# Middle weights of three outer products put by during attention, one piece per unit, instead of during the projections

## The chip, the cores and the metric

The kernel runs on one core of a Trainium2 chip. Its five engines each work through their own queue of instructions in order: TensorE (PE in the profile, PEld for its weight loads), VectorE (DVE), ScalarE (ACT), GpSimd (POOL) and SyncE (SP), which here only issues transfers. An instruction that has to wait holds up all that is queued behind it on its engine. The metric is device time in microseconds; three executions of the kernel before took 2657.4 to 2658.61 us, with a median of 2658.37 us.

## The reference

A transformer layer in float32 for 4 sequences of 512 tokens of width 1024: layer norm, then attention with 32 query heads in 8 groups (a bias by the square root of the distance, a causal mask) and, beside it, a linear layer with a routed low-rank part. Both are added to the input.

```python
x = hidden_states                                    # 4 x 512 x 1024
xn = _layernorm(x)
qkv = xn @ w_qkv                                     # 32 q heads, 8 k, 8 v, of 128
scores = einsum('bqhgd,bkhd->bhgqk', q, k) * scale + bias    # bias is -inf above the diagonal
attn = softmax(scores)
out = einsum('bhgqk,bkhd->bqhgd', attn, v).reshape(B, S, NH * D) @ w_o
lin = xn @ W.T + b
lora = the one of four low ranks (8, 16, 32, 64) that the gate picks for the token
return x + out + lin + lora
```

## The kernel before

The large products are not computed directly: each is cut into 2 x 2 blocks, and Winograd's form of Strassen's scheme makes 7 products of 8, at the price of sums of blocks before and after. In the projections this is done twice (7 outer products, each of 7 inner ones), in the last stage three times: outer, middle and inner. The work has three stages, one after another on TensorE:

- **projections** (to about 1121 us): for two pairs of sequences, 12 sets of columns each (`sets`: a k and v set, then two q sets), every set through its seven outer products. `item` is one outer product of one set; its seven inner products are the steps `m1` to `m7` of `Inner`, driven by `run`, which calls `beside` after each.
- **attention** (to about 1838 us): 32 units, one for a pair, a group of heads and a sequence. Tile rows `i` = 3, 2, 1, 0 of 128 queries have 512, 384, 256 and 128 keys to see. While unit n's probabilities are transposed and weighed with the values, the scores of unit n + 1 are made.
- **last stage**: `w_o` and the linear layer as one product, 7 outer times 7 middle products, `order` naming them as (outer, middle). Outer products are taken in the order 1, 2, 6, 5, 3, 7, 4.

The last stage needs sums of weight blocks. Those for the outer and middle level are made during the projections and put by in DRAM. One **piece** is a tile `wr` of four blocks of 128 x 256 (512 KB): it is loaded, four subtractions in a chain change it in place, and it is stored. There are 40 pieces of the outer level (keys `(kp, e, j)`, stored in `t_d`) and 70 of the middle level (keys `(kp, i)`, stored in `m_d[i]`, 10 for each outer product `i`). A middle piece of outer product 7, 4, 6 or 5 (`SUMMED`) is read from `t_d`, so it comes after the outer pieces; one of 1, 2 or 3 is read from the weights. The list `pieces` (L749 to L753) is shared by three generators `weights_put_by(turn)` (L756), each with a buffer `wr0`, `wr1`, `wr2`. The pieces alternate between GpSimd and VectorE. Loads are issued on ScalarE's queue, stores on SP's. Each `beside()` in the projections gives each of the three one step, in sets for which `pace[3]` is true. `pause(8)` therefore means eight steps between load and first subtraction, `pause(4)` four between last subtraction and store, and `pause(6)` six before the next load. GpSimd's own work there is the inner weights `ti` (L531), four subtractions before an inner product, and the sums over `r` (L582); VectorE's is reading the products out of PSUM (L130) and the sums of blocks.

In attention, `scores(u, i)` (L1004) does for each of four heads: a matmul into one of three banks of PSUM (`psc`, L1012), on VectorE a fused scale, bias and row minimum (`p`, `low`, L1017), on ScalarE the exponential (L1021). Then come the reciprocal (L1024) and, on GpSimd, the scaling of `p` (L1026). `transpose_probs` (L1032) transposes 128 x 128 blocks (`ptr`, L1037) and copies them out as `pt`, every other copy on VectorE (L1040). `weigh` (L1045) makes `po` (L1050). Unit n also loads `k`, `q` and `vT` of unit n + 2 (`load`, L965). Sums of the attention outputs for the last stage run beside: `outer_sums` (L1058) makes `os`, `middle_sums` (L1084) makes `ot`, and they are stored on SP's queue in `s_d` (L1103, L1104, L1114, L1116, L1117). `aside(steps, times)` (L1126) advances such a list by so many steps. In the unit loop (L1146) the calls stand at fixed places. `front[0]` (L1153), six units before the end, issues the first loads of the last stage (L1244, L1260, L1261).

In attention the order on TensorE and SP follows the program, as far as a transfer's buffer is free; that of the other engines is made by the scheduler, except that `pin` keeps what it is given in program order.

Of the kernel before, what the change touches and what calls it, by code (L numbers as in the profile page):

```python
# [23 lines left out]
G = NH // NKV  # L24
# [29 lines left out]
OUTER = (1, 2, 6, 5, 3, 7, 4)  # L54
# [5 lines left out]

SLOT = {1: 0, 7: 1, 2: 2, 4: 3, 5: 4, 6: 5, 3: 6}
SUMMED = {5: 0, 7: 1, 4: 2, 6: 3}


@with_exitstack
def kernel(
# [13 lines left out]
    nc = tc.nc  # L80
    B, S, H = x.shape
# [271 lines left out]
    def project(attention):  # L353
# [5 lines left out]
        with pool("a") as sb, tc.tile_pool(name="stats", bufs=2, reuse_waits="tile") as stats:  # L359
# [390 lines left out]
            for kp in range(2 * KB):  # L750
                if kp + 1 < 2 * KB:
                    pieces += [(kp + 1, e, j) for e in range(2) for j in range(2)]
                pieces += [(kp, i) for i in OUTER]  # L753
            put_by, taken = set(), {}

            def weights_put_by(turn):  # L756

                def load(key):  # L760
                    w = buf(f"wr{turn}", "wr_" + "_".join(str(k) for k in key))
                    if len(key) == 3:
                        kp, e, j = key
                        v = w.rearrange("p (k c) n -> p k c n", k=2)
                        for c in range(2):
                            pin(nc.scalar.dma_start(
                                out=v[:, :, c], in_=rows_of(kp, ds(c * S + j * HS, HS))[:, :, e]
                            ))
                    else:
                        kp, i = key  # L770
                        if i in SUMMED:
                            src = t_d[:, SUMMED[i], :, :, kp].rearrange("p e j n -> p (e j) n")
                            pin(nc.scalar.dma_start(out=w, in_=src))
                        else:
                            k, c = {1: (0, 0), 2: (1, 0), 3: (1, 1)}[i]
                            pin(nc.scalar.dma_start(
                                out=w.rearrange("p (e j) n -> p e (j n)", e=2),
                                in_=rows_of(kp, ts(c, S))[:, k],
                            ))
                    return w  # L780

                def busy(eng):

                    held = pace[2] > pace[4] if eng is GP else own_sums()
                    return held or taken.get(eng, -9) > pace[2] - 2

                yield from pause(9 * turn)
                for n in range(turn, len(pieces), 3):
                    key, eng = pieces[n], (GP, V)[n % 2]
                    if len(key) == 2 and key[1] in SUMMED:  # L790
                        while not put_by >= {(key[0], e, j) for e in range(2) for j in range(2)}:
                            yield
                    w = load(key)
                    yield from pause(8)
                    for k, u, v in ((0, 1, 0), (1, 3, 1), (3, 3, 0), (2, 2, 3)):
                        while busy(eng):
                            yield
                        taken[eng] = pace[2]
                        pin(sub(eng, w[:, k], w[:, u], w[:, v]))
                        yield  # L800
                    yield from pause(4)
                    if len(key) == 3:
                        kp, e, j = key
                        dst = t_d[:, :, e, j, kp]
                    else:
                        kp, i = key
                        dst = m_d[i][:, :, kp]
                    pin(nc.sync.dma_start(out=dst, in_=w))
                    put_by.add(key)
                    yield from pause(6)  # L810

            def once(f, *args):
                f(*args)
# [2 lines left out]
            def pause(n):  # L816
                for _ in range(n):
                    yield
# [122 lines left out]
    def attend(front, begin):  # L941
# [3 lines left out]
        with ExitStack() as stack:  # L945
            sb, sq = None, early.__enter__()
            units = [(p, h, bi) for p in range(NP) for h in range(NKV) for bi in range(2)]
            sizes = {"dist": (S,), "q": (G, S), "k": (S,), "vT": (S,), "bias": (G, S)}
            counts = {"q": 2, "k": 2, "vT": 2, "v": 2, "pt": 10, "o": 4, "ot": 2}
            for i in (3, 2, 1, 0):  # L950
                sizes[f"p{i}"] = (G, (i + 1) * P)
                counts[f"p{i}"] = 2
            sizes.update(v=(NT, D), pt=(S,), os=(3, 2, S), o=(G, S), ot=(9, HS))
            queries = ("dist", "q", "k", "vT", "bias")

            def buf(tag, name):
                where = sq if tag in queries else sb
                return where.tile([P, *sizes[tag]], F32, tag=tag, name=name, bufs=counts.get(tag, 1))
# [6 lines left out]
            def load(u, queue=nc.sync):  # L965
                p, h, bi = u
                n = label(u)
                K[u] = buf("k", f"k_{n}")
                Q[u] = buf("q", f"q_{n}")
                VT[u] = buf("vT", f"vT_{n}")  # L970
                queue.dma_start(out=K[u], in_=k_d[2 * p + bi, h - h % 2][:, h % 2])
                queue.dma_start(out=Q[u], in_=q_d[2 * p + bi, h])
                queue.dma_start(out=VT[u], in_=v_d[2 * p + bi, h - h % 2][:, h % 2])
# [145 lines left out]
            def pause(n):  # L1119
                for _ in range(n):  # L1120
                    yield
# [4 lines left out]
            def aside(steps, times):  # L1126
                while steps and times:
                    times -= 1
                    if next(steps[0], True):
                        steps.popleft()  # L1130

            fill = iter(())
            for u in units[:2]:
                load(u)
# [11 lines left out]
            for n, u in enumerate(units):  # L1146
                p, h, bi = u
                nxt = units[n + 1] if n + 1 < len(units) else None
                after = units[n + 2] if n + 2 < len(units) else None
                if after:  # L1150
                    load(after)
                if n == len(units) - 6:
                    front[0]()  # L1153
                if not nxt:
                    early.__exit__(None, None, None)
                    front[1](O[p, h, 0])
                    fill = begin()
                if bi == 1:
                    beside.append(middle_sums(p, h, (1, 2), "o", O[p, h, 0], True))
                for i in (3, 2, 1, 0):  # L1160
                    if nxt:
                        scores(nxt, i)
                    if i > 1:
                        aside(outer, 1)
                    aside(below, 2)
                    if i < 2 or not nxt and i < 3 or n == close - 2 and i == 2:
                        aside(beside, 2)
                    if i < 2:
                        weigh(u, i + 2)
                        if i == 0 and not nxt:  # L1170
                            outer_sums(p, h, slice(HS, S))
                        next(fill, None)
                    transpose_probs(u, i)
                    next(fill, None)
                    if i == 2 and nxt:
                        values(nxt)
                    if i == 3:
                        aside(outer, 1)
                    if not nxt:
                        if i == 3:  # L1180
                            aside(beside, 2)
                        if i == 2:
                            while beside:
                                aside(beside, 1)
                        if i < 2:
                            front[3 - i]()
                if after and after[2] == 0:
                    distances(after)
                aside(beside, 2)
                weigh(u, 1)  # L1190
                next(fill, None)
                weigh(u, 0)
                if n == close:

                    while beside:
                        aside(beside, 1)
                for _ in fill:
                    pass
                if bi == 1:
                    if n + 1 == close:  # L1200
                        o = O[p, h, 1]
                        outer.append(outer_steps(p, h))
                        aside(outer, 1)
                        t = OS[p, h]
                    else:
                        o, t = outer_sums(p, h, slice(0, HS if (p, h) == last else S))
                        beside.append(pause(3))
                        for k in range(2):
                            O.pop((p, h, k))
                        OS.pop((p, h))  # L1210
                    below.append(middle_sums(p, h, (7, 4), "o", o, False))
                    beside.append(middle_sums(p, h, (5, 6, 3), "os", t, False))
            aside(beside, 9)
            aside(below, 9)
            assert not (beside or below)

    def rows_of(kp, col):

# [506 lines left out]
```

## Time and profile before

| | us |
|---|---|
| median of three executions | 2658.37 |
| the profiled execution | 2657.69 |
| its span, from first to last instruction | 2655.9 |
| DVE `wr<-wr` in the projections | 110 + 110 rows at 128x256, mean 0.645 |
| POOL `wr<-wr` in the projections | 110 + 110 rows at 128x256, mean 0.786 |
| POOL `ti_q<-w_q` at 128x256 | 0.827 mean |
| TensorE, all instructions | busy 2600.1 |

The 220 rows of each engine are two groups of 110 that the page adds up. The first subtraction of a piece starts at 118.2 us and the last at 1088.0 us. The granted TensorE clock is 0.996 over the span. Bytes over the span: 392.72 MB read and 261.10 MB written, 246 GB/s. The issue table of the page gives the median time from issue to landing: 4.6 us for `m<-wr`, 3.7 for `t<-wr`, 6.7 for `wr<-t` and 5.7 for the 512 KB `wr<-in_w_o_dram`.

A row of a timeline is: start us, us, engine, line, operation, tiles written `<-` read, shape, count, and in brackets the idle time of the engine before it and what ended it. A row of stages is: from:to us, its length, then for PE, PEld, DVE, ACT and POOL the busy time and number of instructions, the granted clock, the share of the DMA engines and GB/s. A row of waits is: who waited for whom, us in total, times, longest. Lines are those of the kernel before.

### The profile page before, as it was taken

The numbers are of one execution on the slowest core, as the hardware profiler recorded it, in microseconds if no ns is written. First come the engines' busy times: TensorE is split into PE (matmuls) and PEld (weight loads), VectorE is DVE, ScalarE is ACT, GpSimd is POOL, SyncE is SP. The second block draws the span as 40 slices with busy tenths as digits, with TensorE's granted clock in tenths as the row PEclk, the third lists the DMA queues.
The fourth block names the chain that finished last, engine by engine and source line by source line (L and its number), as shares of the span: only waits on it lengthen the run. The fifth ranks groups of instructions, "written<-read, shape, count | busy, mean of one in ns | idle before, by whom it ended". The sixth has DMA issues, their size and how long they took to land.

```text
span 2655.9 us, 35975 instructions
## 1 busy us (share of the span) xinstructions
PE 2600.1 (98%) x11872; PEld 2074.8 (78%) x11872; DVE 1797.7 (68%) x3654; ACT 652.1 (25%) x1730; POOL 1921.4 (72%) x1976
## 2 busy tenths in 40 slices
PE   7899999999999999999999999999999999999999
PEld 7788888888888888866666666665788888888887
DVE  6876776778676767566666666666766666666574
ACT  3011111100000000276666666675000000000000
POOL 2588787877798989667777778675765567755593
PEclk9999999999999999999999999999999999999999
DMA  4379897858876767336666575766987888878884
GB/s 139 104 264 310 281 349 230 295 193 315 286 256 205 264 223 254 129 102 208 226 205 226 186 229 188 226 238 223 363 287 285 301 293 327 283 277 311 308 319 175
DMA packets 386570, 656.19 MB, mean 247 GB/s; under 512 B 22441, under 2 KB 291113, under 8 KB 376274
## 3 DMA queue, kind: packets, MB, share of 16 engines
q1 hardware_dynamic: 314322, 566.47, 61.5%
q10 hardware_dynamic: 70752, 82.85, 9.6%
q0 software_dynamic: 1312, 4.59, 0.5%
q8 instruction: 95, 1.56, 0.2%
q14 instruction: 89, 0.73, 0.1%
HBM read 392.72 MB, written 261.10 MB: 246 GB/s over the span
## 4 chain that ended last, share of the span: by engine, by line
PE 65%; POOL 4%; DVE 3%; DMA 3%; issue 1%; SPq 1%; ACT 0%; POOLq 0%; ACTq 0%; DVEq 0%
PE pc L1308 15%; PE psc L1012 9%; PE po L1050 8%; PE pd L1308 8%; PE pc_q L553 6%; PE pa L1308 4%; PE pc_kv L553 3%; PE ptr L1037 3%; PE pd_q L553 3%; PE pd_kv L553 2%; PE pa_q L553 1%; DMA s<-os 1%; DVE p L1017 1%; DVE pt L1040 1%; PE pa_kv L553 1%
## 5 line engine op out<-in xcount | busy, mean ns | idle before, releaser
L1026 POOL TENSOR_SCALAR p<-p,tot 128x256 f32<-128x256 f32 (+3 forms) x512 | 319.8, 643 | 139.4 <-DVE tot L1024 89.0
L1012 PE MATMUL psc<-k,q 128*128 128x512 f32 (+3 forms) x1024 | 306.3, 437 | 3.0 <-DVE low L1017 1.7
L1017 DVE CUSTOM_DVE_ANT_0 p<-psc,bias 128x256 f32<-128x256 f32 (+3 forms) x512 | 244.7, 491 | 93.3 <-PE psc L1012 70.4
L1021 ACT ACTIVATE p<-p,low 128x256 f32<-128x256 f32 (+3 forms) x512 | 284.4, 557 | 74.7 <-DVE low L1017 63.0
L1050 PE MATMUL po<-pt,v 128*128 128x512 f32 x640 | 290.9, 593 | 0.7 <-DVE pt L1040 0.7
L133 POOL TENSOR_TENSOR t<-w 128x640 f32<-128x640 f32 x95 | 183.1, 1927 | 134.4 <-DMA w<-m 60.6
L1012 PEld LDWEIGHTS psc<-k,q 128*128 128x128 f32 x1024 | 172.5, 190 | 102.5 <-issue 54.5
L133 POOL TENSOR_TENSOR t<-w,t 128x640 f32<-128x640 f32 x95 | 196.0, 2063 | 35.2 <-PE pc L1308 31.4
L1037 PEld LDWEIGHTS ptr<-ident,p 128*128 128x128 f32 x1280 | 147.5, 141 | 71.4 <-issue 39.0
L1050 PEld LDWEIGHTS po<-pt,v 128*128 128x128 f32 x640 | 116.7, 190 | 109.7 <-issue 99.5
L133 POOL TENSOR_TENSOR wr<-wr 128x256 f32<-128x256 f32 x220 | 172.5, 786 | 32.8 <-DMA wr<-in_w_o_dram 10.4
L1040 DVE COPY pt<-ptr 128x512 f32<-128x512 f32 x192 | 130.0, 684 | 76.0 <-PE ptr L1037 74.1
L1037 PE MATMUL ptr<-ident,p 128*128 128x128 f32 x1280 | 167.6, 274 | 4.4 <-DVE pt L1040 3.0
L553 PE MATMUL pc_q<-xi,ti_q 128*128 128x256 f32 x640 | 166.6, 383 | 3.1 <-DVE q L130 2.0
L168 ACT COPY m<-pc 128x256 f32<-128x256 f32 x30 | 11.2, 373 | 564.3 <-PE pc L1308 560.0
L133 POOL TENSOR_TENSOR ti_q<-w_q 128x256 f32<-128x256 f32 x128 | 105.9, 827 | 58.7 <-PE pc_kv L553 35.4
L133 DVE TENSOR_TENSOR wr<-wr 128x256 f32<-128x256 f32 x220 | 141.9, 645 | 6.1 <-DMA s<-xo 3.1
L553 PEld LDWEIGHTS pc_q<-xi,ti_q 128*128 128x128 f32 x640 | 120.2, 191 | 24.4 <-issue 7.5
L553 PE MATMUL pd_q<-xi,ti_q 128*128 128x256 f32 x448 | 116.1, 381 | 7.1 <-POOL ti_q L133 7.1
L168 ACT COPY q<-pc_q 128x256 f32<-128x256 f32 x64 | 23.8, 373 | 359.6 <-PE pc_q L553 311.2
L1308 PE MATMUL pc<-sa,w 128*128 128x256 f32 x480 | 112.1, 381 | 0.0
L1308 PE MATMUL pd<-s,w 128*128 128x256 f32 x480 | 111.5, 379 | 0.0
(343 smaller groups left out, 6016.8 us busy)
## 6 DMA issues: line engine op xcount, KB each, us to landing
sa<-s SPq DMA_DIRECT2D x98, 640.0 KB, 7.9
s<-ot SPq DMA_DIRECT2D x107, 384.0 KB, 4.8
m<-wr SPq DMA_DIRECT2D x70, 512.0 KB, 4.6
w<-m SPq DMA_DIRECT2D x28, 1280.0 KB, 7.1
w_q<-in_w_qkv_dram SPq DMA_DIRECT2D x16, 2048.0 KB, 12.4
q<-q SPq DMA_DIRECT2D x32, 1024.0 KB, 7.2
s<-os SPq DMA_DIRECT2D x45, 512.0 KB, 4.7
t<-wr SPq DMA_DIRECT2D x40, 512.0 KB, 3.7
```

The source lines that it names most:

```text
L133: return eng.tensor_tensor(dst, u, v, ALU.subtract)
L168: nc.scalar.copy(dst, src)
L553: nc.tensor.matmul(dst, ops_w[m][:, c, :], XI[i][m][:, c, :], start=start and c == 0, stop=c == 1, skip_group_check=True,)
L1012: nc.tensor.matmul(sc[:, :n], Q[u][:, g, ts(i, P)], K[u][:, :n], start=True, stop=True)
L1017: nc.vector.tensor_tensor_reduce(pr[:, g], sc[:, :n], bias[p, h][:, g, S - n :], -SCALE, BIG, ALU.add, ALU.min, low,)
L1021: nc.scalar.activation(pr[:, g], pr[:, g], AF.Exp, bias=low, scale=-1.0, accum_out=tot[:, g : g + 1])
L1026: nc.gpsimd.tensor_scalar(pr[:, g], pr[:, g], tot[:, g : g + 1], 1.0, ALU.mult, ALU.mult)
L1037: nc.tensor.transpose(tr[:, ts(g, P)], PR[u, i][:, g, ts(j, P)], ident)
L1040: nc.vector.tensor_copy(pt, tr)
L1050: nc.tensor.matmul(po, V[u][:, j, :], PT[i, j], start=(j == 0), stop=(j == i))
L1308: nc.tensor.matmul(bk, w[:, k], x[:, k], start=start and k == 0, stop=stop and k == KB - 1, skip_group_check=True,)
```

## The change

The thirty middle pieces of outer products 3, 7 and 4 leave the list of the projections. A new generator makes them in attention, all on VectorE, with one buffer `wr` of its own, its loads and stores both on SP's queue. It is stepped six times in each of the first 31 units: once after `load` (the load), twice after the transposes of tile row 1 and twice after those of tile row 0 (the four subtractions), and once at the end of the unit (the store). The 80 pieces that stay in the projections still go by turns to three generators, with pauses of 14, 5 and 10 steps in place of 8, 4 and 6.

```diff
+LATE = (3, 7, 4)
...
-                pieces += [(kp, i) for i in OUTER]
+                pieces += [(kp, i) for i in OUTER if i not in LATE]
...
                     w = load(key)
-                    yield from pause(8)
+                    yield from pause(14)
...
-                    yield from pause(4)
+                    yield from pause(5)
...
-                    yield from pause(6)
+                    yield from pause(10)
...
-            sizes = {"dist": (S,), "q": (G, S), "k": (S,), "vT": (S,), "bias": (G, S)}
+            sizes = {"dist": (S,), "q": (G, S), "k": (S,), "vT": (S,), "bias": (G, S), "wr": (4, HS)}
...
-            queries = ("dist", "q", "k", "vT", "bias")
+            queries = ("dist", "q", "k", "vT", "bias", "wr")
...
+            def late_weights():
+
+                for kp, i in [(kp, i) for i in LATE for kp in range(2 * KB)]:
+                    w = buf("wr", f"wr_{kp}_{i}")
+                    if i in SUMMED:
+                        src = t_d[:, SUMMED[i], :, :, kp].rearrange("p e j n -> p (e j) n")
+                        nc.sync.dma_start(out=w, in_=src)
+                    else:
+                        nc.sync.dma_start(
+                            out=w.rearrange("p (e j) n -> p e (j n)", e=2), in_=rows_of(kp, ts(1, S))[:, 1]
+                        )
+                    yield
+                    for k, s, t in ((0, 1, 0), (1, 3, 1), (3, 3, 0), (2, 2, 3)):
+                        pin(sub(nc.vector, w[:, k], w[:, s], w[:, t]))
+                        yield
+                    nc.sync.dma_start(out=m_d[i][:, :, kp], in_=w)
+                    yield
+
+            pieces = deque([late_weights()])
...
                     load(after)
+                if nxt:
+                    aside(pieces, 1)
...
                     transpose_probs(u, i)
+                    if nxt and i < 2:
+                        aside(pieces, 2)
...
                 for _ in fill:
                     pass
+                if nxt:
+                    aside(pieces, 1)
```

More of the change, by code (lines that the diff above doesn't have):

```diff
@@ L1214, in attend @@
             aside(below, 9)
-            assert not (beside or below)
+            assert not (beside or below or pieces)
     def rows_of(kp, col):
```

## The prediction

> **What bounds the kernel now.** I read the shares of busy time first, then the busy time by stage, then who waited for whom in each stage, and last the timeline of single units.
>
> ```profile
> span 2655.9 us, 35975 instructions
> PE 2600.1 (98%) x11872; PEld 2074.8 (78%) x11872; DVE 1797.7 (68%) x3654; ACT 652.1 (25%) x1730; POOL 1921.4 (72%) x1976
> 133.00:598.00 465.00, 455.74 (x2187) 395.17 (x2185) 341.92 (x729) 61.63 (x133) 382.76 (x473) 1.00 0.81 274
> 598.00:1121.00 523.00, 515.41 (x2365) 447.06 (x2364) 359.79 (x722) 40.28 (x103) 437.77 (x544) 1.00 0.71 243
> 1121.00:1838.00 717.00, 709.63 (x3002) 433.59 (x3001) 487.10 (x1459) 490.11 (x1361) 528.03 (x628) 1.00 0.62 201
> ```
>
> TensorE is the bound everywhere: it idles 9.3 + 7.6 = 16.9 us in the projections from 133 us on, and 7.4 us in attention. So the change can win at most some 17 us, plus matmuls that are stretched without showing as idle; whatever it puts before a matmul in attention is lost in full. VectorE is busy 68% of attention, with gaps of about 7 us in a unit of 22.8 us. Who holds TensorE up in the projections:
>
> ```profile
> PE pd_q L553 <- POOL ti_q L133: 7.1, 9, 1.3
> PE pd_q L553 <- DVE q L130: 2.1, 4, 0.7
> PE pc_q L553 <- DVE q L130: 2.0, 4, 0.7
> ```
>
> [...]Half is GpSimd making the inner weights late, half VectorE reading PSUM late.
>
> **Gain in the projections.** In the changed program's own order a set of projections holds 8 piece subtractions on GpSimd where there were 11 or 12, and 8 on VectorE where there were 11 or 12: 160 each instead of 220. I walked the timeline back from each of the 31 idle stretches of TensorE over 0.06 us between 133 and 1121 us (16.7 us in sum). About 10 us have a piece's subtraction among the last instructions ahead of the one waited for; about 6 us are led by the sums over `r` or the outer sums, which stay. Of the 10 us, three stretches (0.86, 0.97, 0.64 us at 672, 674 and 686) follow a subtraction that itself stood waiting for a transfer:
>
> ```profile
> 668.96 2.33 POOL L133 TENSOR_TENSOR wr<-wr 128x256 f32<-128x256 f32 x3 [4.80 <-DMA wr<-t]
> 672.02 1.13 PE L553 MATMUL pd_q<-xi,ti_q 128*128 128x256 f32 x4 [0.86 <-POOL ti_q L133]
> ```
>
> A pause of 14 steps instead of 8 between load and first subtraction takes these away: 2.5 us. The other 7.5 us shrink with the count, by 60/220: 2.0 us. Each such stall also stretches its matmuls by 0.1 to 0.3 us (1.13 against 1.03 for four), about 1.5 us in all. Gain **6 us**; from 2 (waits only move) to 12 (most go). The 30 loads that ACT no longer issues free 30 x 0.37 us of an engine busy 25%: nothing. The weights concerned are first read at the 29th of 49 last-stage items, some 450 us after attention: being stored later costs nothing.
>
> **Cost in attention: the order on VectorE.** Thirty pieces of four subtractions are 120 x 0.41 to 0.67 us = 50 to 80 us. That VectorE has room for it (230 us idle) says little, since it works in order. The changed order puts the first subtraction right after the copy `pt` of tile row 1 and before the first minimum of the four `i = 0` score heads, the second after that minimum, the last two after the unit's last `pt`. At the first place:
>
> ```profile
> 1444.60 0.69 DVE L1040 COPY pt<-ptr 128x512 f32<-128x512 f32 x1 [0.63 <-PE ptr L1037]
> 1444.83 1.27 PE L1012 MATMUL psc<-k,q 128*128 128x128 f32 x8
> 1445.26 0.29 DVE L1017 CUSTOM_DVE_ANT_0 p<-psc,bias 128x128 f32<-128x128 f32 x1
> 1448.52 0.60 PE L1037 MATMUL ptr<-ident,p 128*128 128x128 f32 x4
> ```
>
> Scores have three banks, so the fourth head needs the first head's minimum done. Eight matmuls that flow take 0.28 + 7 x 0.107 = 1.03 us (four transposes of the same width: 0.60 = 0.28 + 3 x 0.107); these take 1.27, in the units between 1.38. The fourth head is thus **already waiting** for VectorE, with no slack, in every unit: what stands before that minimum moves TensorE one for one. Engines overlap successive instructions by some 0.08 us, and in every second unit VectorE has 0.08 us to spare, so a subtraction of 0.41 us delays by 0.2 to 0.35 us.
>
> Here a rule speaks against the change. The Trainium skill, "SBUF — State Buffer", section "Who interferes with whom": a VectorE instruction with two SBUF inputs contends with a GpSimd instruction that reads SBUF, and the later one blocks for the whole of the other. GpSimd is scaling `p` (128x384 or 128x256) at this point in 26 of 32 units. The trace agrees in the projections: pieces on VectorE average 0.417 us with GpSimd idle (23) and 0.67 us beside its two-input work (196). Beside scaling by 128x128 a 128x512 sum of attention takes 0.727 us against 0.679 alone. By that row the delay stays near 0.3 us, 9 us in all; by the rule half of a 0.6 us scaling comes on top, 0.55 us, 16 us. I take 0.4 us: 30 x 0.4 = **12 us**, kept between 6 and 17.
>
> The second subtraction is covered: ScalarE paces what follows (four exponentials, 0.39 us apart, against 0.22 us of minima). The last two have 1.49 or 0.84 us of VectorE idle before the next unit's first minimum, and its fourth head another 0.8 us: nothing, at worst 0.2 us in half the units.
>
> **The new wait: landing.** That first subtraction also waits for the piece's load, and everything in VectorE's queue, hence the fourth head, waits behind it. The load waits for the previous piece's store to land (one buffer). In SP's new order the store of one unit kind stands behind four stores and before `k` and `q`: it is issued at about 1455, lands at 1460, the load lands by 1466, the subtraction stands at 1468: in time. In the other kind it stands late:
>
> ```profile
> 1477.20 1.19 SPq L972 DMA_DIRECT2D q<-q  x1
> 1478.49 0.93 SPq L1104 DMA_DIRECT2D s<-o  x2
> 1479.51 1.26 SPq L1103 DMA_DIRECT2D s<-o  x2
> 1484.67 0.33 SPq L973 DMA_DIRECT2D vT<-v  x1
> 1488.00:1490.00 2.00, 2.00 (x9) 0.99 (x8) 1.65 (x2) 0.16 (x1) 1.90 (x2) 1.00 0.00 0
> ```
>
> The store goes between L1104 and L1103, at 1479.5, into queues that are full at 333 to 344 GB/s until 1486; half a megabyte adds 1.5 us. It lands at about 1486.5, the load is issued then, and the subtraction is due at 1490.9. The page's issue table gives 4.6 us for `m<-wr` and 6.7 for `wr<-t` under load; the shortest here is 3.2. "DMA: Bandwidth & Descriptors", section "Anatomy of one DMA", fits 2.0 us + bytes / 436 kB per us (for GpSimd's path): 3.2 us, lands at 1489.7, no wait; by 4.6 us it lands at 1491.1, 0.2 us late; by 6.7, 2.3 us late. As the queues have just run dry I stay near the first two: 14 units x 0.15 = **2 us**; ends 0 and 14 x 2 = 28. `vT`, queued behind this load, is due a unit later: free.
>
> Near the end of attention SP runs late and last-stage loads fill the queues. At 1757 store, `k`, `q` and `vT` precede the load, which then lands near 1767.5, due at 1765.3: 2 us. Two units on, SP's new order puts the load behind six stores of `os` and `ot` that before are issued from 1805 to 1811.7:
>
> ```profile
> 1808.66 1.39 SPq L1116 DMA_DIRECT2D s<-os  x1
> 1810.09 1.56 SPq L1117 DMA_DIRECT2D s<-ot  x1
> ```
>
> It is issued at about 1812.5 and, behind a backlog (the last store took 7.9 us), lands near 1819; the subtraction is due at 1811.4. That is 7 to 8 us, of which 2 us fall on a wait that VectorE has there anyway. Together **8 us**, from 0 to 12. The last-stage loads, moved behind a piece's load from 1714 to about 1739, are needed after 1838: nothing.
>
> **Sum.** -6 + 12 + 2 + 8 = +16 us. The profiled execution took 2657.7 us (span 2655.9), 0.7 below the median of 2658.4; so about **2674 us**, its own range 2664 to 2684.
>
> **Rivals.** (1) *The pieces fit VectorE's gaps and the projections run free*: for it, 230 us idle in attention; then gains of 6 to 12 us stand alone against at most 4: 2650. Against it, the 1.27 us row. Chance 0.10. (2) *Draw*: the subtraction delays 0.25 us (7 us), all loads land, the projections give 8: 2658. Chance 0.15. (3) *Landing decides*: in every second unit the load comes 1.5 us late, so 12 + 21 + 10 - 6 = +37: 2695. It decides from a load time above 4.4 us on, and `wr<-t` has 6.7. Chance 0.20. Or the freed slots give nothing in the projections, since waits move to the sums over `r`: 2680, inside the forecast's range. Forecast 0.55.
>
> Measurement tells about 0.2% (5.3 us) from no change. Faster 0.10, same 0.15, slower 0.75. The range runs from the draw to rival 3, 2655 to 2695.
>
> **What would show it.** TensorE idle in the projections falls from 16.9 to 11 to 13 us. In attention the eight 128x128 score matmuls take about 1.7 us, and VectorE's `wr` rows wait for `DMA wr` little except in the last four units. Attention lengthens by some 20 us. If the score row stays near 1.3 us, my main step is wrong; if `wr` waits for DMA in every second unit, rival 3 is right.

## The result, and the profile after

The changed kernel takes 2667.87 us (median of six executions, 2665.2 to 2670.49), the kernel before, run beside it, 2657.89 us (2654.64 to 2662.27). The ratio is 1.0036, with a 95% interval of 1.0023 to 1.0049: **slower**, by less than half a per cent but clear of 1, and by 10 us where 16 were forecast. The profiled execution's span is 2666.6 us, 10.7 us above that of before.

The head of the page, then the rows by stage in the windows used for before:

```profile
span 2666.6 us, 35927 instructions
PE 2601.0 (98%) x11872; PEld 2078.4 (78%) x11872; DVE 1813.8 (68%) x3714; ACT 654.9 (25%) x1730; POOL 1874.1 (70%) x1916
133.00:598.00 465.00, 457.57 (x2200) 397.60 (x2199) 325.36 (x705) 61.84 (x133) 354.67 (x441) 1.00 0.72 240
598.00:1121.00 523.00, 520.03 (x2393) 452.35 (x2392) 353.41 (x710) 46.81 (x119) 418.46 (x529) 1.00 0.64 218
1121.00:1838.00 717.00, 694.24 (x2930) 423.21 (x2929) 517.10 (x1538) 479.43 (x1323) 518.92 (x609) 1.00 0.73 242
```

TensorE's busy total is the same within 1 us, so the shares tell nothing; the rows by stage do. In the two rows up to 1121 us it idles 7.4 + 3.0 = 10.4 us where it idled 16.9; in attention it idles 22.8 us where it idled 7.4. Who it waits for, first in the projections, then in attention (1121 to 1850 us), and last the row of the kernel before for the same wait in attention:

```profile
PE pd_q L555 <- POOL ti_q L135: 3.3, 5, 1.2
PE pc_q L555 <- DVE q L132: 2.0, 3, 0.9
```

```profile
PE psc L1014 <- DVE low L1019: 18.2, 32, 3.7
PE ptr L1039 <- DVE pt L1042: 2.9, 15, 0.2
```

```profile
PE psc L1012 <- DVE low L1017: 1.7, 3, 0.9
```

The wait for GpSimd's `ti_q` has halved from 7.1. The new wait is that of a score matmul for VectorE's row minimum: once for each of the thirty pieces, one of these as long as 3.7 us, and two at the end that the kernel before has as well. One unit of the middle, all engines but with most lines left out, shows the place:

```profile
1371.82 2.61 POOL L1028 TENSOR_SCALAR p<-p,tot 128x384 f32<-128x384 f32 x4
1371.92 0.69 DVE L1042 COPY pt<-ptr 128x512 f32<-128x512 f32 x1 [2.34 <-PE ptr L1039]
1372.16 0.83 PE L1014 MATMUL psc<-k,q 128*128 128x128 f32 x6
...
1372.53 0.70 DVE L135 TENSOR_TENSOR wr<-wr 128x256 f32<-128x256 f32 x1
1373.16 0.28 DVE L1019 CUSTOM_DVE_ANT_0 p<-psc,bias 128x128 f32<-128x128 f32 x1
...
1373.50 0.49 PE L1014 MATMUL psc<-k,q 128*128 128x128 f32 x2 [0.51 <-DVE low L1019]
```

Three heads' matmuls (six) flow; those of the fourth (two) stand 0.51 us until the first head's minimum is done, and that stood behind the piece's subtraction. The eight matmuls that took 1.27 us in the prediction's unit now take 1373.99 - 1372.16 = 1.83 us. The subtraction takes 0.70 us, not the 0.41 of one that is alone, and GpSimd is scaling `p` all the while.

Where the 10.7 us come from, read at fixed matmuls of the two traces:

| stretch on TensorE | before, us | after, us | change |
|---|---|---|---|
| start to the set of projections that begins near 112 us | 111.52 | 114.51 | +3.0 |
| from there to the last matmul of the projections | 1011.08 | 999.81 | -11.3 |
| first to last score matmul | 716.63 | 735.40 | +18.8 |
| last score matmul to the end | 818.57 | 818.76 | +0.2 |

The third stretch begins 1.9 us before the second ends, in both kernels. The first row has nothing to do with the change: it is the clock, and is told under the hardware below.

### The profile page after: what moved, and what is told of

It reads as the page before. It is cut to its first block, busy times and chain, and to the rows that moved or that the text cites. A ratio compares the mean times of both kernels' runs of the same rounds, so it can differ in the third digit from the quotient of the medians.

```text
span 2666.6 us, 35927 instructions
## 1 busy us (share of the span) xinstructions
PE 2601.0 (98%) x11872; PEld 2078.4 (78%) x11872; DVE 1813.8 (68%) x3714; ACT 654.9 (25%) x1730; POOL 1874.1 (70%) x1916
## 4 chain that ended last, share of the span: by engine, by line
PE 69%; DVE 3%; DMA 2%; issue 1%; POOL 0%; SPq 0%; ACT 0%; DVEq 0%; ACTq 0%; POOLq 0%
PE pc L1336 15%; PE po L1052 10%; PE psc L1014 9%; PE pd L1336 8%; PE pc_q L555 7%; PE pa L1336 4%; PE pd_q L555 3%; PE pc_kv L555 3%; PE ptr L1039 3%; PE pa_q L555 2%; PE pd_kv L555 2%; DVE p L1019 1%; DVE pt L1042 1%; PE pa_kv L555 1%; PE ptr_v L1003 1%
## 5 line engine op out<-in xcount | busy, mean ns | idle before, releaser
L1028 POOL TENSOR_SCALAR p<-p,tot 128x256 f32<-128x256 f32 (+3 forms) x512 | 328.4, 662 | 162.8 <-DVE tot L1026 107.6
L1014 PE MATMUL psc<-k,q 128*128 128x512 f32 (+3 forms) x1024 | 306.9, 437 | 18.7 <-DVE low L1019 18.2
L135 DVE TENSOR_TENSOR wr<-wr 128x256 f32<-128x256 f32 x280 | 164.3, 587 | 4.6 <-DMA wr<-t 3.6
L135 POOL TENSOR_TENSOR wr<-wr 128x256 f32<-128x256 f32 x160 | 124.8, 780 | 6.4
L135 POOL TENSOR_TENSOR ti_q<-to_q 128x256 f32<-128x256 f32 x96 | 72.0, 750 | 63.8 <-PE pc_q L555 61.5
L135 POOL TENSOR_TENSOR ti_q<-w_q,ti_q 128x256 f32<-128x256 f32 x128 | 113.1, 883 | 5.0
```

The lines of the kernel that those rows point to most:

```text
L135: return eng.tensor_tensor(dst, u, v, ALU.subtract)
L1014: nc.tensor.matmul(sc[:, :n], Q[u][:, g, ts(i, P)], K[u][:, :n], start=True, stop=True)
L1028: nc.gpsimd.tensor_scalar(pr[:, g], pr[:, g], tot[:, g : g + 1], 1.0, ALU.mult, ALU.mult)
```

## The experiments

All runs were timed beside the kernel before. It took 2659.9 us (2652.95 to 2664.31) beside the two other places, the run without subtractions and the one with the old pauses; 2659.64 (2654.55 to 2662.38) beside the two doses and the run without late pieces; and 2659.51 (2652.02 to 2664.98) beside the other three. Each was profiled once. "Attention" is the time from the first to the last score matmul; "pitch" is the mean distance of the units 3 to 28, measured from one unit's first score matmul to the next one's: 22.85 us in the kernel before, 23.30 in the changed one.

**Is it the order? Two other places for the first two subtractions.** In the first run they are made after the first head's minimum:

```diff
-            def scores(u, i):
+            def scores(u, i, between=lambda: None):
...
+                    if g == 0:
+                        between()
...
-                        scores(nxt, i)
+                        scores(nxt, i, (lambda: aside(pieces, 2)) if i == 0 else lambda: None)
...
-                    if nxt and i < 2:
+                    if nxt and i < 1:
                         aside(pieces, 2)
```

> The same 120 subtractions, loads and stores; only the first pair of each unit stands one place later on VectorE: behind the first head's minimum instead of ahead of it. Theory A (order: what stands ahead of the first minimum of the 128-key scores holds up the fourth head's matmul): the eight 128x128 score matmuls go back from 1.7 us with a stall to about 1.3 us, a unit gets 0.4 us shorter, 28 units give 12 us: attention about 723 us instead of 735, the kernel about 2655 to 2657 us. Theory B (amount: VectorE and GpSimd block each other, wherever the subtractions stand): nothing changes, 2667. Theory C (the added megabyte of transfers per unit): nothing changes, 2667.

In the second they come once all of the 128-key row's minima and its reciprocal are done:

```diff
                         scores(nxt, i)
+                        if i == 0:
+                            aside(pieces, 2)
...
-                    if nxt and i < 2:
+                    if nxt and i < 1:
                         aside(pieces, 2)
```

> The first pair stands behind all four minima of the 128-key scores and the reciprocal, ahead of the last pt copy of the unit. Theory A: as in the run before for the score matmuls, and the load has 2 us more to land, so that the one late unit near the end costs 1 to 2 us instead of 4; but in every second unit the pt copy now stands behind two sums and two subtractions and may come late for the last weighing, 0 to 0.5 us in 15 units. 2652 to 2662 us. Theories B and C: 2667.

The first took 2655.88 us, ratio 0.9989 (0.9978 to 1.0000), hardly told from the kernel before; attention 722.4 us, pitch 22.84. The second took 2655.10 us, ratio 0.9975 (0.9966 to 0.9985), **faster than both kernels**; attention 719.3, pitch 22.86. TensorE's waits in attention in the second:

```profile
PE ptr L1039 <- DVE pt L1042: 2.9, 15, 0.2
PE psc L1014 <- DVE low L1019: 2.0, 3, 0.9
PE po L1052 <- DVE pt L1042: 1.7, 2, 1.1
```

The 18.2 us are gone, with as many subtractions and transfers as in the changed kernel. Here is how little their own duration matters at a good place:

```profile
1370.66 0.18 DVE L1026 RECIPROCAL tot<-tot 128x4 f32<-128x4 f32 x1 [0.84 <-ACT p L1023]
1370.75 1.91 DVE L135 TENSOR_TENSOR wr<-wr 128x256 f32<-128x256 f32 x2
```

The two take 1.91 us here, beside two-input sums on GpSimd, against 0.8 alone, and the pitch does not show it: nothing that TensorE needs soon is queued behind them. So the place is the cause of the regular delay, and the amount and the transfers are not. What the first variant still loses is the last piece, whose load is late by 4.47 us:

```profile
1808.99 0.43 DVE L135 TENSOR_TENSOR wr<-wr 128x256 f32<-128x256 f32 x1 [4.47 <-DMA wr<-t]
1813.22 1.10 PE L1054 MATMUL po<-pt,v 128*128 128x512 f32 x2 [3.43 <-DVE pt L1044]
```

**A miss: no subtractions at all.** This was meant to have only the transfers in attention:

```diff
-                        pin(sub(nc.vector, w[:, k], w[:, s], w[:, t]))
```

> Leaves out the 120 subtractions in attention; the pieces are still loaded and stored at the same places of SP's queue (what is stored is the raw blocks). Theory A: attention goes back to about 717 us, the kernel to about 2649 us. Theory B: the same, 2649. Theory C: attention stays near 735 us, the kernel near 2667.

It took 2709.26 us, ratio 1.0185 (1.0171 to 1.0199). The waits of SyncE's queue and of TensorE in attention say why:

```profile
SPq L1148 <- DMA wr<-t: 60.1, 14, 6.8
SPq L1140 <- DMA m<-wr: 42.5, 13, 5.6
...
PE psc L1014 <- DMA q<-q: 23.9, 5, 8.5
PE psc L1014 <- DVE low L1019: 16.3, 9, 4.2
```

With no arithmetic between load and store, the planned order of SyncE's queue put load, store and load of pieces next to each other. SyncE then stood for each landing, `q` queued behind it came late, and TensorE waited 8.5 us at worst. How the other 16.3 us, behind VectorE's minima, come about was not followed. The run tests nothing of what it was made for; it shows what a transfer that waits costs when it stands ahead of one that is needed.

**The dose.** So the subtractions were kept, with their waits and places, and only shortened: to one column, and to half of the columns.

```diff
-                        pin(sub(nc.vector, w[:, k], w[:, s], w[:, t]))
+                        pin(sub(nc.vector, w[:, k, :1], w[:, s, :1], w[:, t, :1]))
```

```diff
-                        pin(sub(nc.vector, w[:, k], w[:, s], w[:, t]))
+                        pin(sub(nc.vector, w[:, k, :HS // 2], w[:, s, :HS // 2], w[:, t, :HS // 2]))
```

> The changed kernel with each of the 120 late subtractions cut to one column (128x1 in place of 128x256): this leaves out nearly all of their arithmetic, and keeps every load, store, wait and the order of all queues. Theory A (the time of the first subtraction ahead of the first 128-key minimum is what attention pays): the fourth score head flows again but for a fixed cost of an instruction of some 0.06 us; unit pitch about 22.9 us, attention 718 to 723 us, of which 3 to 6 are the last piece's late landing; total about 2652. Theory C (the 30 MB of loads and stores in attention is what it pays): attention stays at 735, total 2668. A mixture would lie between.

> As the run with one column, but each late subtraction works on 128 of the 256 columns: half of the arithmetic left out, all queues and waits as in the changed kernel. A dose test. Theory A: a subtraction of 128x128 takes about 0.2 us, so the fourth score head waits about half as long, 0.2 to 0.25 us a unit: attention 724 to 729 us, total about 2659 to 2662, midway between the run with one column and the changed kernel. If the cost were a step that does not depend on the length (a switch or block of VectorE by GpSimd), attention would stay at 733 to 736; if it were the transfers, likewise.

One column: 2659.25 us, ratio 0.9999 (0.9990 to 1.0008), attention 727.9. Half: 2661.98 us, ratio 1.0013 (1.0004 to 1.0022), attention 728.8. Theory C, attention at 735 us whatever the length, falls: the transfers cost TensorE time only where a load is late (0.85 us in one unit of the middle and some 4.4 us in the last two of the run with one column). Theory A holds in direction, and in the second run in size, but one column was to cost next to nothing and costs over two fifths of the full subtraction. The first subtraction of a unit, from the three timelines, in the units where GpSimd is scaling beside it and in those few where it is not:

| columns | alone, us | beside scaling (median), us | pitch over before, us |
|---|---|---|---|
| 1 | 0.155 | 0.402 | 0.20 |
| 128 | 0.282 | 0.528 | 0.33 |
| 256 | 0.416 | 0.661 | 0.45 |

(In the run with one column one load was late in unit 15; its 0.85 us are taken out of the pitch.) Each step of 128 columns costs TensorE 0.12 to 0.13 us, what it costs VectorE. In every row TensorE loses the subtraction's duration less 0.20 to 0.21 us: so much VectorE has to spare here. In the durations beside scaling lie 0.25 us that have nothing to do with length. A unit of the middle, VectorE and then GpSimd, in the run with one column:

```profile
1370.31 0.69 DVE L1042 COPY pt<-ptr 128x512 f32<-128x512 f32 x1 [2.34 <-PE ptr L1039]
1370.92 0.42 DVE L135 TENSOR_TENSOR wr<-wr 128x1 f32<-128x1 f32 x1
1371.27 0.28 DVE L1019 CUSTOM_DVE_ANT_0 p<-psc,bias 128x128 f32<-128x128 f32 x1
```

```profile
1370.19 2.27 POOL L1028 TENSOR_SCALAR p<-p,tot 128x384 f32<-128x384 f32 x4
```

An instruction of one column stands 0.42 us. The minimum behind it, which reads one of its inputs from PSUM, takes its usual 0.28 beside the same scaling.

**What the fixed part is.** Each late subtraction was replaced by a sum along one block, which reads one input from SBUF instead of two:

```diff
-                        pin(sub(nc.vector, w[:, k], w[:, s], w[:, t]))
+                        pin(nc.vector.tensor_reduce(w[:, k, :1], w[:, s], mybir.AxisListType.X, ALU.add))
```

> The changed kernel with each of the 120 late subtractions replaced by a sum along one block of the piece (128x256 read, 128x1 written; the subtractions' results are left out): an instruction of VectorE with one input in SBUF instead of two, in the same place of every queue, with the same waits and transfers. It asks about the fixed part of the cost: beside GpSimd's scaling of the probabilities the first subtraction takes 0.25 us longer whatever its length (0.15, 0.28 and 0.415 us alone, 0.40, 0.53 and 0.66 us beside it). Theory D (the two engines share a way to SBUF that an instruction with two inputs there needs): the replacement takes its time alone, some 0.3 to 0.45 us, in all units, attention gets some 0.25 us a unit shorter than in the changed kernel, 726 to 729 us, total 2658 to 2661. Theory E (anything else at that place, such as the start of an instruction after the copy out of PSUM): the 0.25 us stay, attention 733 to 736, total 2666 to 2669.

It took 2663.81 us, ratio 1.0018 (1.0008 to 1.0029); attention 728.6, pitch 23.05. The total is 3 us above what theory D expected, attention within it (its last load was late by 3.6 us, as in the changed kernel). The view of the tile decides: duration of the shortest, the median and the longest of the 120, in ns.

```profile
L1147 DVE TENSOR_REDUCE wr<-wr x120: 403/410/420, 1139.8 to 1819.9; 128x1 f32<-128x256 f32 x120
```

and of the changed kernel's subtractions:

```profile
L135 DVE TENSOR_TENSOR wr<-wr x120: 411/459/705, 1139.9 to 1826.9; 128x256 f32<-128x256 f32 x120
```

Same place, same length alone, GpSimd as busy (515.9 us of the 717 against 518.9): with one input no instance is stretched, with two they go up to 705 ns. That the sum writes one column only is not the reason, since the subtraction of one column was stretched. So the fixed part is the meeting of a two-input instruction with GpSimd's scaling, and the cost of 0.45 us a unit is **0.20 us of length and 0.25 us of that meeting**.

The traces also say what sets the 0.25 us. A late subtraction that starts while GpSimd is busy, with 0.16 us or more of GpSimd's instruction left, ends a set time after that instruction does: by 0.27 us for 256 columns (all 71 of the changed kernel, 0.266 to 0.273), by 0.14 us for 128 (all 66, 0.134 to 0.141), by 0.003 to 0.009 us for one column (56 of 58; the other two 0.04). The sum with one input ends anywhere from 0.12 us before to 0.23 us after. So the subtraction stands until GpSimd's running instruction is done. For the first one of a unit 0.40 us of the scaling are left in the median; the set time is 0.15 us shorter than the subtraction alone, and 0.40 - 0.15 = 0.25. It is fixed only because each unit reaches this place at about the same point of a scaling.

**The two halves of the gain in the projections.** The changed kernel with the pauses of before, and the changed kernel without the thirty late pieces:

```diff
-                    yield from pause(14)
+                    yield from pause(8)
...
-                    yield from pause(5)
+                    yield from pause(4)
...
-                    yield from pause(10)
+                    yield from pause(6)
```

> The changed kernel with the pauses of before (8, 4, 6) for the 80 pieces that stay, which are then done earlier and as densely as before. Of the 8 us that the projections gained, the prediction gave the pauses 2.5 of 6, the count the rest. If the fewer pieces give the gain, the projections end 4 to 6 us before 1122.6 us and the kernel takes 2669 to 2672; if the pauses give it, they end within 2 us of 1122.6 and the kernel takes 2674 to 2676.

```diff
-            pieces = deque([late_weights()])
+            pieces = deque()
...
-                pin(self.queue.dma_start(out=w, in_=m_d[i][:, SUMMED[m]]))
+                pin(self.queue.dma_start(out=w, in_=m_d[{3: 1, 7: 2, 4: 6}.get(i, i)][:, SUMMED[m]]))
```

> The changed kernel without the thirty late pieces at all (no load, subtraction or store; the last stage reads other middle weights of the same size in their place, so its traffic is unchanged and its results are not the reference's). It is the gain in the projections alone. By the traces it should be 8.3 us under the kernel before, about 2649.5, with attention at 716 to 717 us and a projections end near 1114.5. If the gain in the projections is partly given back later, whatever attention carries (such as a lower granted clock), it lies above 2652.

With the old pauses: 2675.11 us, ratio 1.0056 (1.0044 to 1.0069). From the set near 112 us to the last matmul the projections take 1007.7 us, against 1011.1 before and 999.8 in the changed kernel: the smaller count is worth 3.4 us, the longer pauses, for which it makes room, 7.9. What the pauses take away stands in GpSimd's waits in the projections, first before, then with the old pauses; the last row is TensorE's wait for the inner weights with the old pauses:

```profile
POOL wr L133 <- DMA wr<-in_w_o_dram: 10.4, 6, 5.5
POOL wr L133 <- DMA wr<-t: 5.4, 2, 4.8
```

```profile
POOL wr L135 <- DMA wr<-in_w_o_dram: 9.9, 5, 5.5
POOL wr L135 <- DMA wr<-t: 5.5, 2, 3.8
POOL wr L135 <- DMA t<-wr: 4.4, 1, 4.4
```

```profile
PE pd_q L555 <- POOL ti_q L135: 6.3, 7, 1.7
```

With the long pauses GpSimd has no such row: no piece stands at the head of its queue for its landing, and TensorE's wait for the inner weights behind it is 3.3 us. Without the late pieces the kernel takes 2648.66 us, ratio 0.9957 (0.9945 to 0.9970), 11.0 us under the kernel before, and attention takes 715.9: nothing of the gain is given back there. In its profile the stretch from the last score matmul to the end is 2.6 us longer than in that of the kernel before (821.2 against 818.6).

**The last piece held back.** The better order, with the last of the thirty pieces kept in the projections:

```diff
+HELD = {(9, 4)}
...
-                pieces += [(kp, i) for i in OUTER if i not in LATE]
+                pieces += [(kp, i) for i in OUTER if i not in LATE or (kp, i) in HELD]
...
-                    yield from pause(14)
+                    yield from pause(12)
...
-                for kp, i in [(kp, i) for i in LATE for kp in range(2 * KB)]:
+                for kp, i in [(kp, i) for i in LATE for kp in range(2 * KB) if (kp, i) not in HELD]:
```

> The better order (first two subtractions after the reciprocal of the 128-key row) with one more edit: the last of the thirty pieces, the one whose load comes late behind the stores of the last sums, stays in the projections (81 pieces there, pause of 12 instead of 14 steps so that they fit). Expected: the 3 us that the last two units still lose there go to under 1 us, the projections give back 0.5 to 1 us; total 1 to 2.5 us under the same order with all thirty pieces, about 2653. If the tail's loss comes from the sums themselves and not from the piece, nothing changes.

> The better order again, on the same chip as the run with one piece held, as its base: 2655, ratio to the kernel before 0.997 to 0.9985.

2653.29 us with the piece held, ratio 0.9976 (0.9967 to 0.9985); 2654.17 us without, ratio 0.9979 (0.9968 to 0.9989). The better order's lead over the kernel before is confirmed. The edit's own effect is not: by the traces its last two units are 1.9 us shorter and its projections 0.8 us longer, and a difference of 1 us is below what these runs can tell.

So the better order keeps some 5 of the 11 us that the projections win. In its two profiles attention is 2.7 and 4.7 us longer than in the kernel before, of which 2.5 and 3.0 us fall on the last two units, and the stretch from the last score matmul to the end is 4.0 and 1.4 us longer. That last stretch is longer in the run without late pieces too, so the late pieces need not be its cause; it was not followed further.

## Why the prediction was right, and where its sum was off

| term | forecast, us | measured, us |
|---|---|---|
| gain in the projections | -6 | -11.3 |
| first subtraction ahead of the minimum | +12 | +13.2 |
| regular landings | +2 | 0 |
| last units | +8 | +5.6 |
| not in the sum: start, last stage | 0 | +3.2 |
| total | +16 | +10.7 |

Part of the nearness is luck. Of the +10.7 us of these two profiles 3.0 are the clock at the start, which the change does not set; the four terms of the forecast come to +7.5, about half of 16. By the medians of six executions each the change is +10.0, by their interval 6 to 13 us. The direction, and the place and size of the main cost, are not luck: the runs above show them.

- **The order on VectorE** was right in place and size: fourth head already waiting, one subtraction ahead of the first minimum, 0.4 us forecast and 0.45 measured in each regular unit. Moving that pair by itself removes it, with the same number of subtractions and transfers. The score row, forecast at about 1.7 us, is 1.83.
- **The rule against the row.** The row alone was put at 0.3 us of delay, the rule of the Trainium skill ("SBUF — State Buffer", "Who interferes with whom") at 0.55 with half a scaling on top. Measured are 0.20 without the meeting and 0.45 with it: both estimates were 0.1 us too high, since VectorE had 0.2 us to spare, more than I gave it. But the rule's share, 0.25 us, is nearly the 0.3 that it gave; it was right to add it, and the choice of 0.4 leaned too far to the row. The one-input run is as the rule says, too, and so is the end of a stretched subtraction, a set time after GpSimd's instruction. That half a scaling came near is in part luck: the median was 0.40 us left, less 0.15. The row that I took against it (a sum of 128x512 stretched from 0.679 to 0.727 us beside a scaling of 128x128) came from another instruction at another place.
- **The gain in the projections** is the step that failed in size. Idle time was to fall by 4.5 us (2.5 by the pauses, 2.0 by the count) and fell by 6.5, to 10.4, just under the 11 to 13 forecast (by 6.9 in the table's stretch: 16.9 to 9.9). Stretched matmuls were put at 1.5 us, and the remaining 4.4 us are theirs. The starts of the matmuls show it. Flowing ones start 0.216 us apart and the trace gives each 0.379 us, so that the first 0.16 us of a wait does not count as idle. Before, 108 of that stretch's 4650 or so matmuls start over 0.02 us later than this pitch and the idle time shown explain, by 11.8 us together; in the changed kernel it is 71, by 7.4 us. Split the other way, the pauses were undervalued most: I gave them only the three stretches directly behind a late landing, and they are worth 7.9 us.
- **Regular landings** came in time, as the prediction expected at the lower end: VectorE's `wr` waits for a transfer twice in attention, 3.6 us in all, of which 3.37 us are for the last piece. Rival 3, late in every second unit, did not happen.
- **The last units** behave as described. SyncE issues the last piece's load at 1812.2 us behind six stores, VectorE waits for it, and TensorE for VectorE:

```profile
1812.18 1.34 SPq L1140 DMA_DIRECT2D wr<-t  x1
```

```profile
1819.90 0.42 DVE L135 TENSOR_TENSOR wr<-wr 128x256 f32<-128x256 f32 x1 [3.37 <-DMA wr<-t]
```

```profile
1820.59 0.49 PE L1014 MATMUL psc<-k,q 128*128 128x128 f32 x2 [3.68 <-DVE low L1019]
```

  The last two units together are 6.5 us longer, 0.9 of it the regular delay. The load landed by 1819.9 us, where 1819 was forecast, but the subtraction was due at 1816.5 and not at 1811.4, since this unit's 128-key scores began 5.1 us later than before (1816.1 against 1811.0). The earlier unit, forecast 2 us late, was in time. About 1.7 us of the 5.6 are a term that the prediction did not have: the clock was halved after this stall.
- **Rivals 1 and 2** needed the subtraction to cost 4 us or 7 us in all. They fell with the row of waits. At the other place the first one's mechanism holds: the pieces do fit VectorE's gaps, and the kernel gets 5 us faster than before.

## What to carry to other kernels

Room on an engine that works in order is a matter of place: look for what is queued behind the new instruction and whether anyone is already waiting for it. The same 120 subtractions made the kernel 10 us slower ahead of the first minimum, and 5 us faster than before behind the reciprocal. A two-input VectorE instruction beside GpSimd work should be priced with what is left of GpSimd's running instruction as well as with its length, and in a shared queue a load must be given time to land before its first user stands at the head.

## What the runs showed of the hardware

**The price of meeting GpSimd is the rest of its running instruction.** With 0.40 us of a scaling left in the median, the first subtraction of a unit is 0.25 us longer, for 1, 128 and 256 columns alike; with one input it is no longer at all. Beside a longer instruction the price is higher. In the better order a unit's second subtraction takes 0.47 us in the 15 units in which only scalings run beside it. It takes 1.38 us in the 14 in which it starts behind a two-input sum of GpSimd, and in all 14 it ends 0.28 us after that sum. There are exceptions: in the run with the pair behind the first minimum 11 of 65 late subtractions end before the GpSimd instruction that was running when they started; in all 11 it had started less than 0.05 us ahead of them. The scaling suffers too, a little: those of 128x384 between 1180 and 1780 us take 0.630 us in the mean in the changed kernel, 0.601 before and 0.587 in the run with one input.

**The clock after a stall.** Windows of the changed kernel around the 3.68 us stall; the granted clock is the third number from the end:

```profile
1820.50:1821.10 0.60, 0.51 (x3) 0.51 (x4) 0.60 (x6) 0.47 (x2) 0.00 (x0) 1.00 0.00 0
1821.10:1824.50 3.40, 3.40 (x5) 1.34 (x5) 1.77 (x7) 1.28 (x7) 1.74 (x3) 0.51 0.01 2
```

For 3.4 us after the stall TensorE ran at half speed, which costs it 1.7 us. Leaving out the run with no subtractions, six runs had one gap of over 1.5 us on TensorE in attention. It was 3.4 to 3.9 us in four, and the clock was halved for 3.4 us after each. Of two shorter ones, that of 2.32 us was followed by the same and that of 2.56 us was not. In the run with no subtractions a gap of 2.03 us was, too. No run without such a gap had it there. The Trainium skill ("TensorE: Matmul & The Clock Gate", "HAM oscillation — how this bites in real kernels") puts the bound at idle gaps of about 3.4 us; here gaps of 2.03 and 2.32 us were enough.

**The start differs from run to run.** The same window of two runs of one kernel, the better order:

```profile
43.40:71.40 28.00, 24.89 (x111) 22.76 (x110) 17.43 (x27) 1.61 (x6) 8.61 (x8) 0.70 0.05 19
```

```profile
43.40:71.40 28.00, 23.86 (x133) 21.34 (x131) 23.64 (x36) 1.61 (x6) 11.56 (x12) 0.94 0.05 19
```

From about 53 us on the clock was halved for 17.1 us in the first and for 3.4 us in the second, and the set near 112 us began at 114.45 and at 108.29 us; their spans are 2654.4 and 2647.6 us. The kernel before had 10.2 us of it in its profile, the changed one 17.1: that is the +3.0 us of the table's first row. The twelve profiles agree: between two fixed matmuls, of which the first starts near 43.5 us, lie 21.6 us with 3.4 us at half the clock, 24.9 (three profiles) with 10.2, 25.7 and 25.8 (two) with 13.7 and 27.6 to 28.2 (six) with 17.1. It is a matter of chance and not of the change: two of the three with 10.2 us have the changed kernel's projections. Two single profiles of this kernel can differ by 6 us before the change has begun to act; only the stretch from a fixed matmul onwards compares them.
